# A conditional residual block on one Trainium2 core: the layer norm's square root in another form, small VectorE operations in another order, and b2 by TensorE in other batches

## The chip, the cores and the metric

The kernel runs on one core of a Trainium2 chip. A core has five engines that run side by side, each with its own instructions in order, and that wait for one another by semaphores: TensorE (PE in the profile, PEld for its weight loads), VectorE (DVE), ScalarE (ACT), GpSimd (POOL) and SyncE (SP), which here only issues transfers between memory and the on-chip buffers. TensorE writes to PSUM, a small memory beside the larger SBUF. The metric is the device time of one execution in microseconds (us), lower is better. "Faster" and "slower" compare the changed kernel with the kernel before.

## What is computed

Input x holds 128 batches of 128 rows of 512 numbers (H), in 32-bit floats. For each batch an id from 0 to 8 picks one of ten sets of weights (the gather below), and a small adapter with a layer norm is added to x:

```python
w1 = W1[language_ids]
w2 = W2[language_ids]
h = jnp.einsum('bsh,bha->bsa', hidden_states, w1) + b1[language_ids][:, None, :]
h = jax.nn.relu(h)
adapted = jnp.einsum('bsa,bah->bsh', h, w2) + b2[language_ids][:, None, :]
x = hidden_states + adapted
mean = jnp.mean(x, axis=-1, keepdims=True)
var = jnp.mean(jnp.square(x - mean), axis=-1, keepdims=True)
normed = (x - mean) * jax.lax.rsqrt(var + LN_EPS)
return normed * gamma[language_ids][:, None, :] + beta[language_ids][:, None, :]
```

The result is x plus what this returns. Both products are in 32-bit floats; A, the width of the adapter, is 128.

## The kernel before

A batch (128 rows on the 128 partitions, 512 columns) is the unit of work. All ten W1 and W2 lie in SBUF from the start, and beta, gamma and b2 are spread over the partitions into `beta_b`, `gamma_b` and `b2_b` by products of a 0/1 column of `pick` with `parts` (the rows in three bfloat16 parts), whose results ACT and DVE copy in turn (`spread`).

The order of every engine's instructions is written out by hand: `keep` ties each instruction to the one issued before it on its engine. A loop over i runs one step per batch. In step i the engines work on different batches:

- PE: `transpose_x(i)` (L197, four 128x128 transposes into `pxT`), `down(i-1)` (L220, four products with the batch's W1 copy `w1s`), `up(i-2)` (L237, the product with W2 into `ys[b]`, a PSUM tile `py`). For a batch with `b2_by_matmul(b)` a product with `pick` ahead of it puts b2 into `py` (L236); before, these are batches 0 to 3 and every b with b % 4 == 1.
- ACT: `copy_xT(i)` (L201), `stage_w1(i+1)` (L192), `relu(i-1)` (L228, gives `hT`), `square(i-3)` (L255, the square of y minus mean with the sum over the row as a second output; it takes `nmean` as bias), and after every second batch `deviation` (L261, the square root of variance plus eps for a pair of batches, `sd`).
- POOL: `add_b2(b+2)` (L207, r = x + b2, for the batches whose b2 is not by TensorE) and `add_beta(b)` (L214, o = x + beta), for b = i-3.
- DVE, for b = i-3: `residual(b)` (L243, y = y + r or y + x, with the row sum), `negative_mean(b)` (L248), and for the pair of batches before: the reciprocal square root in five small operations on two columns (`rstd_1` to `rstd_5`, L266, L270, L273, L276, L281: a Newton step on the reciprocal of sd), `scale` (L287, y minus mean, times gamma), `finish` (L296, y times rstd plus o). An even b carries scale of one batch of the pair, rstd_1 to rstd_3 and the finish of the older pair's second batch; an odd b carries rstd_4, the other scale, rstd_5 and the finish of the pair's first batch.
- SP: one load of four batches of x (1 MB) in every fourth step, and one store of two finished batches (512 KB) in every second, in the order of the program.

The buffers that tie engines together: `pxT` and `ph` one each, `py` five, r four, o five pairs, x four groups of four batches. So `up(b)` needs `finish(b-5)` done, and `transpose_x(i+1)` needs the copy of xT i. Batch numbers become weight addresses through registers, which each engine loads for four batches at a time.

The first steps are written apart: products up of batches 0 and 1 before the loop, of batch 2 in step 4, of batch 3 at the end of step 5, behind `down(4)`. The last five batches (E = 123 and up) go through `tail`, which gives the statistics of each batch by itself (`rstd_of`, L317 to L325, `deviation_of`, `shift`), hands three batches to ACT and POOL (`by_pool`) and finishes the last two on DVE (`finish_last`, L357).

Of the kernel before, what the change touches and what calls it, by code (L numbers as in the profile page):

```python
# [8 lines left out]
FP = mybir.dt.float32  # L9
# [7 lines left out]
P = 128  # L17
# [6 lines left out]
def cond_resid_kernel(ctx: ExitStack, tc: tile.TileContext, x, itok, W1, b1, W2, b2, gamma, beta, out):  # L24
# [102 lines left out]
    both = st.tile([P, R], FP, tag="both", name="both", bufs=1)[:96, :]  # L127
    keep(nc.vector.tensor_tensor(both, ident[:96, 0:R], ident[:96, 32 : 32 + R], ALU.add))
    keep(nc.vector.tensor_tensor(pick, both, ident[:96, 64 : 64 + R], ALU.add))


    wrap = const.tile([1, B], I32, name="wrap")
# [51 lines left out]
        return lids[g, engine][b % G]  # L184

    def b2_by_matmul(b):
        return b < 4 or b % 4 == 1

    def stage_w1(b):
        w1s[b] = wp.tile([P, KC, A], FP, tag="w1s", name=f"w1s_{b}")  # L190
# [39 lines left out]
    def up(b):  # L230
# [6 lines left out]
        keep(nc.tensor.matmul(ys[b], lhsT=hT[b], rhs=w2[:, bass.ds(v * H, H)], start=not m, stop=True))  # L237
        del hT[b]

    def residual(b):  # L240
        r = xb(b) if b2_by_matmul(b) else rs.pop(b)
        s = st.tile([P, 1], FP, tag="sum", name=f"sum_{b}")
        keep(nc.vector.scalar_tensor_tensor(ys[b], ys[b], 1.0, r, ALU.mult, ALU.add, accum_out=s))  # L243
        sums[b] = s

    def negative_mean(b):
        nmeans[b] = st.tile([P, 1], FP, tag="nmean", name=f"nmean_{b}")
        keep(nc.vector.tensor_scalar(nmeans[b], sums.pop(b), -1.0 / H, None, ALU.mult))  # L248
# [8 lines left out]
    sds, y0s, stats = {}, {}, {}  # L257

    def deviation(g):
        sds[g] = st.tile([P, 2], FP, tag="sd", name=f"sd_{g}")  # L260
        keep(nc.scalar.activation(sds[g], ssqs[g], AF.Sqrt, bias=eps, scale=1.0 / H))  # L261


    def rstd_1(g):
        stats[g] = p_s.tile([P, 6], FP, tag="s", name=f"stat_{g}")
        keep(nc.vector.tensor_scalar(stats[g][:, 0:2], ssqs.pop(g), -0.5 / H, -0.5 * EPS, ALU.mult, ALU.add))  # L266

    def rstd_2(g):
        y0s[g] = st.tile([P, 2], FP, tag="y0", name=f"y0_{g}")
        keep(nc.vector.reciprocal(y0s[g], sds.pop(g)))  # L270

    def rstd_3(g):
        keep(nc.vector.tensor_tensor(stats[g][:, 2:4], stats[g][:, 0:2], y0s[g], ALU.mult))  # L273

    def rstd_4(g):
        keep(nc.vector.tensor_tensor(stats[g][:, 4:6], stats[g][:, 2:4], y0s[g], ALU.mult))  # L276

    def rstd_5(g):
        rstds[g] = st.tile([P, 2], FP, tag="rstd", name=f"rstd_{g}")
        keep(  # L280
            nc.vector.scalar_tensor_tensor(rstds[g], stats.pop(g)[:, 4:6], 1.5, y0s.pop(g), ALU.add, ALU.mult)  # L281
        )

    def scale(b):
        v = lid(b, ET.DVE)
        keep(
            nc.vector.scalar_tensor_tensor(  # L287
                ys[b], ys[b], nmeans.pop(b), gamma_b[:, bass.ds(v * H, H)], ALU.add, ALU.mult
            )
        )  # L290

# [19 lines left out]
    def rstd_of(b, n):  # L311

        if not ends:
            ends["t"] = p_s.tile([P, 32], FP, tag="s", name="stat_ends")
        t = ends["t"][:, 8 * (b % 4) : 8 * (b % 4) + 3]
        if n == 1:
            keep(nc.vector.tensor_scalar(t[:, 0:1], ssqs.pop(b), -0.5 / H, -0.5 * EPS, ALU.mult, ALU.add))  # L317
        elif n == 2:
            y0s[b] = st.tile([P, 1], FP, tag="y0", name=f"y0_{b}")
            keep(nc.vector.reciprocal(y0s[b], sds.pop(b)))  # L320
        elif n < 5:
            keep(nc.vector.tensor_tensor(t[:, n - 2 : n - 1], t[:, n - 3 : n - 2], y0s[b], ALU.mult))  # L322
        else:
            rstds[b] = st.tile([P, 1], FP, tag="rstd", name=f"rstd_{b}")
            keep(nc.vector.scalar_tensor_tensor(rstds[b], t[:, 2:3], 1.5, y0s.pop(b), ALU.add, ALU.mult))  # L325

    def deviation_of(b):
        ssq = st.tile([P, 1], FP, tag="ssq", name=f"ssq_{b}")
        sq = tp.tile([P, H], FP, tag="sq", name=f"sq_{b}")
        keep(nc.scalar.activation(sq, ys[b], AF.Square, bias=nmeans[b], accum_out=ssq))  # L330
        sds[b] = st.tile([P, 1], FP, tag="sd", name=f"sd_{b}")
        keep(nc.scalar.activation(sds[b], ssq, AF.Sqrt, bias=eps, scale=1.0 / H))
        ssqs[b] = ssq

    def rstd_col(b):
# [24 lines left out]
    def tail(b):  # L360
        p = E // 2
        if b == E + 3:
            rstd_of(b - 2, 4)
        residual(b)
        if b == E + 1:
            rstd_1(p)
            rstd_2(p)
            negative_mean(b)
            rstd_3(p)
            scale(E - 1)  # L370
            rstd_4(p)
            rstd_5(p)
            shift(E)
            finish(E - 2)
            store(p - 1)
            deviation_of(b)
            by_pool(E, False)
        elif b == E + 2:
            negative_mean(b)
            rstd_of(b - 1, 1)  # L380
            rstd_of(b - 1, 2)
            finish_last(E - 1)
            store_last(E)
            rstd_of(b - 1, 3)
            deviation_of(b)
        elif b == E + 3:
            rstd_of(b - 2, 5)
            negative_mean(b)
            shift(b - 2)
            residual(b + 1)  # L390
            negative_mean(b + 1)
            by_pool(b - 2, False)
            store_last(b - 2)
            rstd_of(b - 1, 1)
            rstd_of(b - 1, 2)
            rstd_of(b - 1, 3)
            scale(b - 1)
            deviation_of(b)
            rstd_of(b - 1, 4)
            rstd_of(b - 1, 5)  # L400
# [6 lines left out]
            rstd_of(b + 1, 1)  # L407
            rstd_of(b + 1, 2)
            rstd_of(b, 3)
            rstd_of(b + 1, 3)  # L410
            scale(b + 1)
            rstd_of(b, 4)
            rstd_of(b + 1, 4)
            rstd_of(b, 5)
            rstd_of(b + 1, 5)
            finish_last(b)
            finish_last(b + 1)

# [42 lines left out]
    for i in range(3, B + U):  # L461
        if i < B and i % G == 0 and i // G + 3 < NG:
            load_x(i // G + 3)
        b = i - U - 1
        if i == 4:
            up(2)
        if i > 3 and on(i):
            transpose_x(i)
        if b <= E:
            add_b2(b + 2)  # L470
            add_beta(b)
        if i > 4 and on(i - 1):
# [12 lines left out]
        p = g - 1  # L485
        mine, old = 0 <= p < B // 2, 0 <= p - 1 < B // 2
        if b == E:
            for n in range(b + 3, B):
                add_b2(n)
            for n in range(b + 1, B):  # L490
                add_beta(n)
        if b > E:
            tail(b)
        elif half == 0:
            if on(b):
                residual(b)
# [12 lines left out]
        else:  # L509
            if on(b):  # L510
                residual(b)
            if mine:
                rstd_4(p)
                scale(2 * p + 1)
                rstd_5(p)
# [49 lines left out]
```

## Time and profile before

| | |
|---|---|
| median of 3 runs | 319.38 us (319.27 to 320.71) |
| the profiled execution | 319.72 us |
| its span, first to last instruction | 318.0 us |
| busy: PE, DVE, ACT, POOL | 302.7, 297.9, 289.1, 280.6 us |
| granted TensorE clock, mean | 0.99 |
| HBM read, written | 38.86 MB, 33.55 MB |

An engine's busy time counts overlapping instructions once; it says how much of the span the engine had something in flight, not whether it could have taken more. The groups of the page that the change touches, with line, engine, operation, tiles (out<-in), shape, count, and after the bar the busy time in us, the mean duration of one in ns, and the engine's idle time just before them with what ended most of it:

```profile
L207 POOL TENSOR_TENSOR r<-x,b_b 128x512 f32<-128x512 f32 x93 | 118.9, 1279 | 20.2 <-DMA x<-in_x_dram 12.3
L255 ACT ACTIVATE sq<-py,nmean 128x512 f32<-128x512 f32 x124 | 85.3, 688 | 6.7 <-DVE nmean L248 4.2
L248 DVE TENSOR_SCALAR nmean<-sum 128x1 f32<-128x1 f32 x128 | 18.7, 146 | 0.2
L236 PE MATMUL py<-parts,pick 96*128 96x512 bf16 x35 | 13.3, 381 | 0.0
L276 DVE TENSOR_TENSOR stat<-stat,y 128x2 f32<-128x2 f32 x62 | 12.7, 205 | 0.0
```

The durations of consecutive instructions of one engine overlap, so the sum of durations is more than the time that the engine needs; the distance from one start to the next is the better measure.

### The profile page before, as it was taken

The page shows a single profiled execution, that of the slowest core. Times are in us where ns is not written, and L with a number is a line of the kernel's source. Part 1 is how long each engine was busy: PE and PEld are TensorE (multiplying, and loading weights), DVE is VectorE, ACT ScalarE, POOL GpSimd, SP SyncE. Part 2 cuts the span into 40 slices and gives each one's busy share as a digit, 9 for nine tenths or more (in the row PEclk, how much of TensorE's full clock was granted, in tenths as well). Part 3 has the DMA queues.
Part 4 walks back from the last instruction along what each step waited for, and adds up shares of the span by engine and source line. Part 5 has one row for each costly group of instructions (what it writes and reads, how often), then busy time and mean ns, then how long its engine had stood idle before and what let it go on. Part 6 is the DMA issues. An engine that isn't in the chain of part 4 may idle for free. (4 is left out here: it accounts for less than half of the span.)

```text
span 318.0 us, 7173 instructions
## 1 busy us (share of the span) xinstructions
PE 302.7 (95%) x1883; PEld 225.0 (71%) x1884; DVE 297.9 (94%) x995; ACT 289.1 (91%) x726; POOL 280.6 (88%) x234
## 2 busy tenths in 40 slices
PE   7989999999999999999999999999999999999950
PEld 3566777777777777777777777777777777777730
DVE  6827999999999999999999999999999999999995
ACT  3977999999999999999999999999999999999971
POOL 1308999999999999999999999999999999999873
PEclk9999999999999999999999999999999999999995
DMA  7998777667776666677776666677766666633333
GB/s 204 318 386 294 205 260 262 233 232 266 260 242 212 215 223 242 228 238 265 261 231 215 209 227 248 223 245 264 258 220 208 222 231 241 219 128 133 132 128 138
DMA packets 41002, 72.88 MB, mean 229 GB/s; under 512 B 1753, under 2 KB 6884, under 8 KB 40962
## 3 DMA queue, kind: packets, MB, share of 16 engines
q1 hardware_dynamic: 40902, 72.38, 67.2%
q8 instruction: 15, 0.25, 0.3%
q14 instruction: 25, 0.20, 0.2%
q10 hardware_dynamic: 60, 0.05, 0.1%
HBM read 38.86 MB, written 33.55 MB: 228 GB/s over the span
## 5 line engine op out<-in xcount | busy, mean ns | idle before, releaser
L214 POOL TENSOR_TENSOR o<-x,beta_b 128x512 f32<-128x512 f32 x128 | 162.1, 1280 | 9.2 <-ACT beta_b L164 9.2
L207 POOL TENSOR_TENSOR r<-x,b_b 128x512 f32<-128x512 f32 x93 | 118.9, 1279 | 20.2 <-DMA x<-in_x_dram 12.3
L220 PE MATMUL ph<-xT,w1s 128*128 128x128 f32 x1024 | 135.6, 275 | 0.7 <-ACT w1s L192 0.5
L237 PE MATMUL py<-w,hT 128*128 x256 | 131.0, 594 | 0.9 <-DMA w<-in_L_cond_W_dram 0.7
L220 PEld LDWEIGHTS ph<-xT,w1s 128*128 128x128 f32 x1024 | 124.6, 192 | 2.8 <-ACT hT L228 1.4
L197 PEld LDWEIGHTS pxT<-ident,x 128*128 128x128 f32 x512 | 63.7, 140 | 66.1 <-issue 45.3
L287 DVE SCALAR_TENSOR_TENSOR py<-py,nmean,gamma_b 128x512 f32<-128x512 f32 x126 | 94.6, 751 | 0.0
L255 ACT ACTIVATE sq<-py,nmean 128x512 f32<-128x512 f32 x124 | 85.3, 688 | 6.7 <-DVE nmean L248 4.2
L296 DVE SCALAR_TENSOR_TENSOR o<-py,rstd,o 128x512 f32<-128x512 f32 x122 | 90.3, 740 | 1.0
L192 ACT COPY w1s<-w 128x512 f32 x128 | 79.5, 622 | 0.2 <-DMA w<-in_L_cond_W_dram 0.2
L201 ACT COPY xT<-pxT 128x512 f32<-128x512 f32 x128 | 73.8, 577 | 5.1 <-PE pxT L197 3.6
L197 PE MATMUL pxT<-ident,x 128*128 128x128 f32 x512 | 76.8, 273 | 0.7 <-ACT xT L201 0.7
L243 DVE SCALAR_TENSOR_TENSOR py<-py,r 128x512 f32<-128x512 f32 x93 | 64.4, 692 | 2.5 <-PE pxT L197 0.9
L228 ACT ACTIVATE hT<-ph,b1T 128x128 f32<-128x128 f32 x128 | 47.6, 372 | 1.2 <-PE ph L220 1.2
L237 PEld LDWEIGHTS py<-w,hT 128*128 128x128 f32 x256 | 41.6, 192 | 4.0 <-issue 2.0
L243 DVE SCALAR_TENSOR_TENSOR py<-py,x 128x512 f32<-128x512 f32 x35 | 24.1, 690 | 4.9 <-PE py L237 4.8
L255 ACT ACTIVATION_READ_ACCUMULATOR sq<-py,nmean 128x1 f32 x124 | 24.8, 200 | 0.0
L261 ACT ACTIVATE sd<-ssq,eps 128x2 f32<-128x2 f32 x62 | 18.3, 296 | 2.1
L248 DVE TENSOR_SCALAR nmean<-sum 128x1 f32<-128x1 f32 x128 | 18.7, 146 | 0.2
L236 PE MATMUL py<-parts,pick 96*128 96x512 bf16 x35 | 13.3, 381 | 0.0
L243 DVE DVE_READ_ACCUMULATOR py<-py,r 128x1 f32 x93 | 13.0, 140 | 0.0
L276 DVE TENSOR_TENSOR stat<-stat,y 128x2 f32<-128x2 f32 x62 | 12.7, 205 | 0.0
(54 smaller groups left out, 113.7 us busy)
## 6 DMA issues: line engine op xcount, KB each, us to landing
out_dram<-o SPq DMA_DIRECT2D x61, 512.0 KB, 3.6
x<-in_x_dram SPq DMA_DIRECT2D x30, 1024.0 KB, 6.0
w<-in_L_cond_W_dram SPq DMA_DIRECT2D x4, 640.0 KB, 6.6
w<-in_L_cond_W_dram SPq DMA_DIRECT2D x2, 1280.0 KB, 11.3
x<-in_x_dram SPq DMA_DIRECT2D x4, 512.0 KB, 8.5
out_dram<-o SPq DMA_DIRECT2D x6, 256.0 KB, 2.4
rows<-in_L_cond_beta_dram ACTq DMA_DIRECT2D x1, 20.0 KB
rows<-in_L_cond_gamma_dram SPq DMA_DIRECT2D x1, 20.0 KB
```

What stands on the lines that cost most here:

```text
L192: keep(nc.scalar.copy(w1s[b].rearrange("p k a -> p (k a)"), src))
L197: keep(nc.tensor.transpose(pxs[b][:, k, :], xb(b)[:, k * P : (k + 1) * P], ident))
L201: keep(nc.scalar.copy(xT[b], pxs.pop(b)))
L207: keep(nc.gpsimd.tensor_tensor(rs[b], xb(b), b2_b[:, bass.ds(v * H, H)], ALU.add))
L214: keep(nc.gpsimd.tensor_tensor(os[g][:, j, :], xb(b), beta_b[:, bass.ds(v * H, H)], ALU.add))
L220: nc.tensor.matmul(phs[b], lhsT=w1s[b][:, k, :], rhs=xT[b][:, k, :], start=(k == 0), stop=(k == KC - 1))
L228: keep(nc.scalar.activation(hT[b], phs.pop(b), AF.Relu, bias=b1T[:, bass.ds(lid(b, ET.Activation), 1)]))
L237: keep(nc.tensor.matmul(ys[b], lhsT=hT[b], rhs=w2[:, bass.ds(v * H, H)], start=not m, stop=True))
L243: keep(nc.vector.scalar_tensor_tensor(ys[b], ys[b], 1.0, r, ALU.mult, ALU.add, accum_out=s))
L255: keep(nc.scalar.activation(sq, ys[b], AF.Square, bias=nmeans[b], accum_out=ssqs[g][:, j : j + 1]))
L287: nc.vector.scalar_tensor_tensor(ys[b], ys[b], nmeans.pop(b), gamma_b[:, bass.ds(v * H, H)], ALU.add, ALU.mult)
L296: nc.vector.scalar_tensor_tensor(o, ys.pop(b), rstds[g][:, j : j + 1], o, ALU.mult, ALU.add)
```

## The change

Five parts.

1. `b2_by_matmul`: from batch 4 to 95 the batches whose number leaves 1, 6 or 11 when divided by 16, in place of every fourth; from 96 on every fourth as before. The other batches get b2 from POOL.
2. `up(3)` is called at the start of step 5, ahead of `transpose_x(5)` and `down(4)`, and no longer at its end.
3. The reciprocal square root takes another form, four operations in place of five: the reciprocal of sd, then (ssq + eps) times it, plus sd (Heron's step for the root, twice the root in all), then the reciprocal of that. The factor of two goes into gamma: the columns of `pick` for gamma are multiplied by 2. The small operations are placed so that a 512-column operation stands between each and its input, where there is one: `rstd_1` right behind the even residual, `rstd_2` behind `scale`, `rstd_3` behind `finish`, `rstd_4` behind the odd residual.
4. `square` takes the row sum as bias and -512 as scale (its result is 512 x 512 times the square of before, which the constants of deviation and rstd account for; `H3` is 512 cubed), so it no longer reads `nmean`. Sums and means of two batches lie in one tile of two columns.
5. In `tail` and ahead of it the same operations stand in another order, and `shift` is an operation with a per-row scalar.

```diff
+    keep(nc.vector.tensor_scalar(pick[:, L : 2 * L], pick[:, L : 2 * L], 2.0, None, ALU.mult))
...
     def b2_by_matmul(b):
-        return b < 4 or b % 4 == 1
+        return b < 4 or (b % 16 in (1, 6, 11) if b < 96 else b % 4 == 1)
...
+    def col(tiles, b):
+
+        return tiles[b // 2][:, b % 2 : b % 2 + 1]
+
     def residual(b):
         r = xb(b) if b2_by_matmul(b) else rs.pop(b)
-        s = st.tile([P, 1], FP, tag="sum", name=f"sum_{b}")
-        keep(nc.vector.scalar_tensor_tensor(ys[b], ys[b], 1.0, r, ALU.mult, ALU.add, accum_out=s))
-        sums[b] = s
+        if b % 2 == 0:
+            sums[b // 2] = st.tile([P, 2], FP, tag="sum", name=f"sum_{b // 2}")
+        keep(
+            nc.vector.scalar_tensor_tensor(ys[b], ys[b], 1.0, r, ALU.mult, ALU.add, accum_out=col(sums, b))
+        )
...
-        keep(nc.scalar.activation(sq, ys[b], AF.Square, bias=nmeans[b], accum_out=ssqs[g][:, j : j + 1]))
+        keep(
+            nc.scalar.activation(
+                sq, ys[b], AF.Square, bias=col(sums, b), scale=-float(H), accum_out=col(ssqs, b)
+            )
+        )
...
-        keep(nc.scalar.activation(sds[g], ssqs[g], AF.Sqrt, bias=eps, scale=1.0 / H))
+        keep(nc.scalar.activation(sds[g], ssqs[g], AF.Sqrt, bias=eps, scale=1.0 / H3))
...
     def rstd_1(g):
-        stats[g] = p_s.tile([P, 6], FP, tag="s", name=f"stat_{g}")
-        keep(nc.vector.tensor_scalar(stats[g][:, 0:2], ssqs.pop(g), -0.5 / H, -0.5 * EPS, ALU.mult, ALU.add))
+        y0s[g] = p_s.tile([P, 6], FP, tag="s", name=f"stat_{g}")
+        keep(nc.vector.reciprocal(y0s[g][:, 0:2], sds[g]))
 
     def rstd_2(g):
-        y0s[g] = st.tile([P, 2], FP, tag="y0", name=f"y0_{g}")
-        keep(nc.vector.reciprocal(y0s[g], sds.pop(g)))
+        t = y0s[g]
+        keep(nc.vector.scalar_tensor_tensor(t[:, 2:4], ssqs.pop(g), EPS * H3, t[:, 0:2], ALU.add, ALU.mult))
 
     def rstd_3(g):
-        keep(nc.vector.tensor_tensor(stats[g][:, 2:4], stats[g][:, 0:2], y0s[g], ALU.mult))
+        t = y0s[g]
+        keep(nc.vector.scalar_tensor_tensor(t[:, 4:6], t[:, 2:4], 1.0 / H3, sds.pop(g), ALU.mult, ALU.add))
 
     def rstd_4(g):
-        keep(nc.vector.tensor_tensor(stats[g][:, 4:6], stats[g][:, 2:4], y0s[g], ALU.mult))
-
-    def rstd_5(g):
         rstds[g] = st.tile([P, 2], FP, tag="rstd", name=f"rstd_{g}")
-        keep(
-            nc.vector.scalar_tensor_tensor(rstds[g], stats.pop(g)[:, 4:6], 1.5, y0s.pop(g), ALU.add, ALU.mult)
-        )
+        keep(nc.vector.reciprocal(rstds[g], y0s.pop(g)[:, 4:6]))
...
-    keep(nc.vector.tensor_tensor(ends[b], nmeans.pop(b), rstd_col(b), ALU.mult))
+    keep(nc.vector.tensor_scalar(ends[b], col(nmeans, b), rstd_col(b), None, ALU.mult))
...
         if i == 4:
             up(2)
+        if i == 5:
+            up(3)
         if i > 3 and on(i):
             transpose_x(i)
...
-        if i > 4 and on(i - U):
+        if i > 5 and on(i - U):
             up(i - U)
...
         if b == E:
-            for n in range(b + 3, B):
-                add_b2(n)
-            for n in range(b + 1, B):
+            add_b2(b + 3)
+            add_beta(b + 1)
+            add_b2(b + 4)
+            for n in range(b + 2, B):
                 add_beta(n)
...
             if on(b):
                 residual(b)
             if mine:
+                rstd_1(p)
                 scale(2 * p)
             if on(b):
                 negative_mean(b)
             if mine:
-                rstd_1(p)
                 rstd_2(p)
...
             if mine:
                 rstd_4(p)
                 scale(2 * p + 1)
-                rstd_5(p)
             if on(b):
                 negative_mean(b)
```

In the tail DVE's order after the change is: residual 124, reciprocal of sd for pair 61, scale 122, rstd_2, mean of 124, finish 121, rstd_3, rstd_4, shift 123, residual 125, reciprocal for 124, mean of 125, second step for 124, finish 122, third step, residual 126, last reciprocal for 124, shift 124, residual 127, reciprocal for 125, mean of 126, second step for 125, mean of 127, scale 125, third step and last reciprocal for 125, scale 126, five steps for 126 and 127, scale 127, the last three steps, finish 126, finish 127.

More of the change, by code (lines that the diff above doesn't have):

```diff
@@ L238, in up @@
         del hT[b]
+    def col(tiles, b):
+        return tiles[b // 2][:, b % 2 : b % 2 + 1]
     def residual(b):
         r = xb(b) if b2_by_matmul(b) else rs.pop(b)
-        s = st.tile([P, 1], FP, tag="sum", name=f"sum_{b}")
-        keep(nc.vector.scalar_tensor_tensor(ys[b], ys[b], 1.0, r, ALU.mult, ALU.add, accum_out=s))
-        sums[b] = s
+        if b % 2 == 0:
[3 more added lines that the diff above has]
+        )
     def negative_mean(b):
-        nmeans[b] = st.tile([P, 1], FP, tag="nmean", name=f"nmean_{b}")
-        keep(nc.vector.tensor_scalar(nmeans[b], sums.pop(b), -1.0 / H, None, ALU.mult))
+        if b % 2 == 0:
+            nmeans[b // 2] = st.tile([P, 2], FP, tag="nmean", name=f"nmean_{b // 2}")
+        keep(nc.vector.tensor_scalar(col(nmeans, b), col(sums, b), -1.0 / H, None, ALU.mult))
     def square(b):
@@ L254, in square @@
         sq = tp.tile([P, H], FP, tag="sq", name=f"sq_{b}")
-        keep(nc.scalar.activation(sq, ys[b], AF.Square, bias=nmeans[b], accum_out=ssqs[g][:, j : j + 1]))
+        keep(
[3 more added lines that the diff above has]
+        )
     sds, y0s, stats = {}, {}, {}
+    H3 = float(H) ** 3
     def deviation(g):
         sds[g] = st.tile([P, 2], FP, tag="sd", name=f"sd_{g}")
-        keep(nc.scalar.activation(sds[g], ssqs[g], AF.Sqrt, bias=eps, scale=1.0 / H))
+        keep(nc.scalar.activation(sds[g], ssqs[g], AF.Sqrt, bias=eps, scale=1.0 / H3))
     def rstd_1(g):
-        stats[g] = p_s.tile([P, 6], FP, tag="s", name=f"stat_{g}")
-        keep(nc.vector.tensor_scalar(stats[g][:, 0:2], ssqs.pop(g), -0.5 / H, -0.5 * EPS, ALU.mult, ALU.add))
+        y0s[g] = p_s.tile([P, 6], FP, tag="s", name=f"stat_{g}")
+        keep(nc.vector.reciprocal(y0s[g][:, 0:2], sds[g]))
     def rstd_2(g):
-        y0s[g] = st.tile([P, 2], FP, tag="y0", name=f"y0_{g}")
-        keep(nc.vector.reciprocal(y0s[g], sds.pop(g)))
+        t = y0s[g]
+        keep(nc.vector.scalar_tensor_tensor(t[:, 2:4], ssqs.pop(g), EPS * H3, t[:, 0:2], ALU.add, ALU.mult))
     def rstd_3(g):
-        keep(nc.vector.tensor_tensor(stats[g][:, 2:4], stats[g][:, 0:2], y0s[g], ALU.mult))
+        t = y0s[g]
+        keep(nc.vector.scalar_tensor_tensor(t[:, 4:6], t[:, 2:4], 1.0 / H3, sds.pop(g), ALU.mult, ALU.add))
     def rstd_4(g):
-        keep(nc.vector.tensor_tensor(stats[g][:, 4:6], stats[g][:, 2:4], y0s[g], ALU.mult))
-    def rstd_5(g):
         rstds[g] = st.tile([P, 2], FP, tag="rstd", name=f"rstd_{g}")
-        keep(
-            nc.vector.scalar_tensor_tensor(rstds[g], stats.pop(g)[:, 4:6], 1.5, y0s.pop(g), ALU.add, ALU.mult)
-        )
+        keep(nc.vector.reciprocal(rstds[g], y0s.pop(g)[:, 4:6]))
     def scale(b):
@@ L287, in scale @@
             nc.vector.scalar_tensor_tensor(
-                ys[b], ys[b], nmeans.pop(b), gamma_b[:, bass.ds(v * H, H)], ALU.add, ALU.mult
+                ys[b], ys[b], col(nmeans, b), gamma_b[:, bass.ds(v * H, H)], ALU.add, ALU.mult
             )
@@ L316, in rstd_of @@
         if n == 1:
-            keep(nc.vector.tensor_scalar(t[:, 0:1], ssqs.pop(b), -0.5 / H, -0.5 * EPS, ALU.mult, ALU.add))
+            keep(nc.vector.reciprocal(t[:, 0:1], sds[b]))
         elif n == 2:
[L319 to L322, printed above, removed]
+            keep(
+                nc.vector.scalar_tensor_tensor(t[:, 1:2], ssqs.pop(b), EPS * H3, t[:, 0:1], ALU.add, ALU.mult)
+            )
+        elif n == 3:
+            keep(nc.vector.scalar_tensor_tensor(t[:, 2:3], t[:, 1:2], 1.0 / H3, sds.pop(b), ALU.mult, ALU.add))
         else:
             rstds[b] = st.tile([P, 1], FP, tag="rstd", name=f"rstd_{b}")
-            keep(nc.vector.scalar_tensor_tensor(rstds[b], t[:, 2:3], 1.5, y0s.pop(b), ALU.add, ALU.mult))
+            keep(nc.vector.reciprocal(rstds[b], t[:, 2:3]))
     def deviation_of(b):
@@ L329, in deviation_of @@
         sq = tp.tile([P, H], FP, tag="sq", name=f"sq_{b}")
-        keep(nc.scalar.activation(sq, ys[b], AF.Square, bias=nmeans[b], accum_out=ssq))
+        keep(nc.scalar.activation(sq, ys[b], AF.Square, bias=col(sums, b), scale=-float(H), accum_out=ssq))
         sds[b] = st.tile([P, 1], FP, tag="sd", name=f"sd_{b}")
-        keep(nc.scalar.activation(sds[b], ssq, AF.Sqrt, bias=eps, scale=1.0 / H))
+        keep(nc.scalar.activation(sds[b], ssq, AF.Sqrt, bias=eps, scale=1.0 / H3))
         ssqs[b] = ssq
@@ L362, in tail @@
         if b == E + 3:
-            rstd_of(b - 2, 4)
+            rstd_of(b - 2, 3)
         residual(b)
@@ L366, in tail @@
             rstd_1(p)
+            scale(E - 1)
             rstd_2(p)
             negative_mean(b)
-            rstd_3(p)
-            scale(E - 1)
-            rstd_4(p)
-            rstd_5(p)
-            shift(E)
             finish(E - 2)
             store(p - 1)
+            rstd_3(p)
             deviation_of(b)
+            rstd_4(p)
+            shift(E)
             by_pool(E, False)
         elif b == E + 2:
+            rstd_of(b - 1, 1)
             negative_mean(b)
-            rstd_of(b - 1, 1)
             rstd_of(b - 1, 2)
@@ L383, in tail @@
             store_last(E)
-            rstd_of(b - 1, 3)
             deviation_of(b)
         elif b == E + 3:
-            rstd_of(b - 2, 5)
-            negative_mean(b)
+            rstd_of(b - 2, 4)
             shift(b - 2)
             residual(b + 1)
-            negative_mean(b + 1)
             by_pool(b - 2, False)
@@ L394, in tail @@
             rstd_of(b - 1, 1)
+            negative_mean(b)
             rstd_of(b - 1, 2)
-            rstd_of(b - 1, 3)
+            negative_mean(b + 1)
             scale(b - 1)
             deviation_of(b)
+            rstd_of(b - 1, 3)
             rstd_of(b - 1, 4)
-            rstd_of(b - 1, 5)
             scale(b)
@@ L407, in tail @@
             rstd_of(b + 1, 1)
+            rstd_of(b, 3)
             rstd_of(b + 1, 2)
-            rstd_of(b, 3)
-            rstd_of(b + 1, 3)
             scale(b + 1)
             rstd_of(b, 4)
+            rstd_of(b + 1, 3)
             rstd_of(b + 1, 4)
-            rstd_of(b, 5)
-            rstd_of(b + 1, 5)
             finish_last(b)
@@ L514, in cond_resid_kernel @@
                 scale(2 * p + 1)
-                rstd_5(p)
             if on(b):
```

## The prediction

> **What bounds the kernel now.** I read the page's busy shares first. Four engines stand at 88 to 95% of the span, so they decide nothing; I went on to the timeline of single engines in the middle of the run, where the distance from start to start tells each engine's pace. PE first (start, duration, line, operation, tiles):
>
> ```profile
> 213.93 0.60 PE L197 MATMUL pxT<-ident,x 128*128 128x128 f32 x4
> 214.37 1.06 PE L220 MATMUL ph<-xT,w1s 128*128 128x128 f32 x8
> 215.26 1.02 PE L237 MATMUL py<-w,hT 128*128 x2
> 216.12 0.60 PE L197 MATMUL pxT<-ident,x 128*128 128x128 f32 x4
> ...
> 220.50 0.60 PE L197 MATMUL pxT<-ident,x 128*128 128x128 f32 x4
> 220.94 1.06 PE L220 MATMUL ph<-xT,w1s 128*128 128x128 f32 x8
> 221.83 0.38 PE L236 MATMUL py<-parts,pick 96*128 96x512 bf16 x1
> 222.05 1.02 PE L237 MATMUL py<-w,hT 128*128 x2
> 222.91 0.60 PE L197 MATMUL pxT<-ident,x 128*128 128x128 f32 x4
> ```
>
> A batch takes 2.19 us (213.93 to 216.12): transpose, product down, product up, each starting where the one before has been issued. A batch with b2 by TensorE takes 2.41 (220.50 to 222.91), so that product costs 0.22. The same two distances come back with hardly an exception from batch 6 to batch 124: PE never waits, so it paces the middle. One batch in four has the product: 3 x 2.19 + 2.41 = 8.98 us for four.
>
> DVE is the second. Two consecutive batches:
>
> ```profile
> 105.08 0.75 DVE L287 SCALAR_TENSOR_TENSOR py<-py,nmean,gamma_b 128x512 f32<-128x512 f32 x1
> 105.74 0.15 DVE L248 TENSOR_SCALAR nmean<-sum 128x1 f32<-128x1 f32 x1
> 105.80 0.15 DVE L266 TENSOR_SCALAR stat<-ssq 128x2 f32<-128x2 f32 x1
> 105.86 0.15 DVE L270 RECIPROCAL y<-sd 128x2 f32<-128x2 f32 x1
> 105.94 0.73 DVE L296 SCALAR_TENSOR_TENSOR o<-py,rstd,o 128x512 f32<-128x512 f32 x1
> ...
> 107.99 0.16 DVE L281 SCALAR_TENSOR_TENSOR rstd<-stat,y 128x2 f32<-128x2 f32 x1
> 108.06 0.14 DVE L248 TENSOR_SCALAR nmean<-sum 128x1 f32<-128x1 f32 x1
> 108.24 0.75 DVE L296 SCALAR_TENSOR_TENSOR o<-py,rstd,o 128x512 f32<-128x512 f32 x1
> ```
>
> An operation of 0.15 us occupies only 0.06 when nothing depends on it, and a big one 0.61 to 0.67. L296 at 108.24 waits for rstd, written at 107.99 to 108.15: 0.18 from nmean, not 0.07. A register load in every fourth batch adds 0.12 (L296 to L243 takes 0.79 there, not 0.67). From residual 32 to residual 36, 95.54 to 104.46, four batches take 8.92: DVE just follows PE, its residuals 0.1 to 0.6 us behind the product.
>
> POOL: from 26.59 to 95.57, without one wait, it makes 56 additions, 1.232 us each from start to start. Four batches need seven, 8.62, so it gains on PE and later waits for a free r buffer. ACT makes an xT copy, a w1s copy, hT, the square and its read in 0.47, 0.52, 0.26, 0.57 and 0.11 to 0.25, with the deviation 0.2 to 0.3 more in every second batch: 8.5 us for four.
>
> At the start PE stands still:
>
> ```profile
> 25.74 0.60 PE L197 MATMUL pxT<-ident,x 128*128 128x128 f32 x4
> 27.01 0.66 PE L197 MATMUL pxT<-ident,x 128*128 128x128 f32 x4 [0.68 <-ACT xT L201]
> 27.50 1.06 PE L220 MATMUL ph<-xT,w1s 128*128 128x128 f32 x8
> 28.40 0.38 PE L236 MATMUL py<-parts,pick 96*128 96x512 bf16 x1
> 28.62 1.02 PE L237 MATMUL py<-w,hT 128*128 x2
> 29.48 0.60 PE L197 MATMUL pxT<-ident,x 128*128 128x128 f32 x4
> ```
>
> At the end the chain of waits runs over DVE alone; its shares by engine on the page, and the last entry of DVE's timeline:
>
> ```profile
> DVE 4%; issue 1%; DVEq 0%
> ...
> 313.11 1.41 DVE L357 SCALAR_TENSOR_TENSOR o<-py,rstd,o 128x512 f32<-128x512 f32 x2 [0.39 <-issue]
> ```
>
> [...]
>
> **The change part by part.**
> (1) b2 by TensorE. In batches 4 to 95 it falls from 23 (every fourth) to 17 (three in sixteen); from 96 on it stays 8. PE saves 6 x 0.22 = 1.33 us, all on the path. POOL gets 6 additions more. Sixteen batches now need 29 of them, 29 x 1.232 = 35.73, and PE 16 x 2.19 + 3 x 0.22 = 35.70: level. POOL starts with r of batch 4 ready 5.3 us before its residual, loses about 0.7 of that to the earlier start in (2), and keeps some 4.5 until batch 96; behind it, with one in four, it gains 0.36 on every four batches. From 25.35 it has 99 r and 126 beta additions: 225 x 1.232 = 277.2, so its betas are done at 302.6, before 304.26 today. Cost nothing; the cover is the 4.5 us, which 169 additions up to batch 96 use up if each takes 0.027 more.
>
> (2) Product up of batch 3. It now stands ahead of transpose 5. PE is free at 26.17, when ACT still copies xT 4 (to 26.96). b2 product 26.17 to 26.39, product up 26.39 to 27.25; transpose 5 moves from 27.01 to 27.25, down 4 from 27.50 to 27.69, issued at 28.58. Transpose 6 needs xT 5, which ACT copies at 27.93 to 28.50 after the deviation, as before: it starts at 28.58 where it was 29.48. Gain 0.90. Does ACT follow? Copy of xT 6 at about 30.0 to 30.57, PE asks at 30.77; xT 7 to 32.82, asked at 32.96. Just; I keep 0.90, between 0 (ACT late) and 1.1. A PE wait for a py buffer near batch 19 (0.23) goes too, since DVE gets slack.
>
> (3) Heron's step on DVE. A pair had seven small operations (two nmean, L266, L270, L273, L276, L281), now six. With the distances of the trace, even batch: residual 0.61, scale behind the reciprocal 0.07, 0.66 to nmean, 0.06, 0.07 to L296, 0.65, 0.07 = 2.19; odd batch: 0.61, 0.07, 0.66, 0.07, 0.67 = 2.08. Sum 4.27, with the register load 4.33, against 4.46. PE needs 4.46 for a pair, so this saves nothing in the middle; it only makes room, 0.13 a pair. The new forms (reciprocal into PSUM, two scalar_tensor_tensor on two columns) are not in the trace; the nearest rows are 0.154 to 0.205, and I take 0.07 of engine time each; at 0.12 the pair is 4.47 and the room is gone.
> The reciprocal now stands right behind the even residual and waits there for the deviation (ACT), with the scale, nmean, L296, and so PE's py buffers, queued behind it. At the tightest (batch 120): hT on ACT at 291.80, square 292.07, deviation done at 293.15; product up 120 ends at 292.51, residual from 292.55 to 292.63, reciprocal possible at 293.16 to 293.24. It meets the deviation within 0.02: no cost. At the start it does wait, to 28.06 for pair 0 and about 32.4 for pair 1, while products are still queued in PSUM; buffers for products 6 and 7 come 0.3 and 0.6 us early.
>
> (4) The square's input. It takes the sum, not nmean, so ACT no longer waits for nmean, some 0.8 us later. Off the path until the tail; scale and bias are operands as before. (5) pick x 2 for gamma: one operation like L129 (0.18), covered by the 0.35 that DVE waits for the rows' DMA at L139; 0.2 if uncovered. (6) add_beta ahead of add_b2 at the end: POOL order alone.
>
> (7) The tail. Today residual 124 starts at 301.73 and the last L357 ends at 314.52: 12.79. The new order by the same distances, from residual 124: scale at 0.68, finish 121 at 1.47, two dependent small ones (0.17 each) and the shift to 2.50, residual 125 at 2.57, finish 122 at 3.45, residual 126 at 4.15, shift 124, residual 127 at 5.0, scale 125 at 5.9, scale 126 at 6.8, scale 127 at 8.1 (behind the deviation of 127, ACT), finish 126 at 9.2, end at 10.6. I add 0.4 for a pause like that before L357 (0.39, issue): 11.0. Saved 1.8, between 0.8 (today's pauses stay, or PE's product 127 comes late) and 2.2. PE delivers product 127 at about 304.1 and DVE asks at 304.2, so it fits.
>
> Sum: 1.33 + 0.90 + 0.2 + 1.8 = 4.2. The profiled execution took 319.72 (span 318.0 and 1.7 around it) and would take 315.5; the median of the runs is 319.38, so 315.2.
>
> **Rivals.**
> A, the forecast (0.68): PE paces, 315.2; own range 314.2 to 316.4.
> B (0.20): the ends give less. ACT is too late for transposes 6 to 8 and the tail keeps its pauses: 1.33 + 0.2 + 0.8 = 2.3, 317.0. For it: two margins of 0.2 or less in (2). Against: each is worked out from unhindered ACT distances.
> C (0.06): POOL becomes the bound. At 1.28 us an addition (the page's mean duration) the 169 up to batch 96 take 8.1 longer; less the 4.5 of slack 3.6 are lost: 318.8. For it: 35.73 against 35.70. Against: 56 additions at 1.232 while DVE was as dense.
> D (0.06), slower: the reciprocal of the even batch waits for the deviation in every pair. 62 pairs; 0.13 of wait are hidden, so from 0.20 on (0.07 x 62 = 4.3) the whole gain is lost, and 0.25 gives 322.6. For it: the two meet within 0.02 at best, and ACT has other work. Against: ACT needs 8.5 where PE takes 8.92, so it stays as early as PE lets it.
> That the change does not do what it says is excluded: the changed kernel's instruction order has the six small operations, product 3 ahead of transpose 5, and the fewer products.
>
> **How the numbers follow.** A and B are faster by over 0.5% (under 317.8; half a per cent is about what the measurement tells from no change): 0.88. C is counted as the same, D as slower. Leaving out the fast end of A, C's far half and D, the range is 314.0 to 317.4.
>
> **What would show it.** Right: transposes 2.19 and 2.41 apart, transpose 6 near 28.6, transpose 124 near 292.3 (294.76 today); POOL almost without waits; residual 124 to the last finish in about 11 us. Wrong: a repeated DVE wait for sd ahead of the reciprocal (D), DVE waiting for r from POOL (C), transposes 6 to 8 waiting for xT (B), or PE waiting for finish.

## The result and the profile after

The changed kernel is slower: median 322.81 us of six runs (322.46 to 325.78) against 319.92 us of six of the kernel before on the same chip (319.27 to 321.06), ratio 1.0105, 95% interval 1.0063 to 1.0148. The forecast was 315.2. The profiled execution is the slowest of the six (325.78 us, span 324.0), so what its lines show is two to three us larger than in the median run. Two kernels below, e8 and e11, ran in two groups of times about 2% apart, the kernel before only in one; where e11 is compared, its lower group is.

The clock is no cause: the granted clock is 1.00 from 16 to 310 us in both profiles. What the profile shows first is that the chain of waits, followed back from the end, has changed its engine. Chain of the changed kernel, shares by engine:

```profile
POOL 44%; PE 29%; issue 12%; DMA 3%; POOLq 3%; SPq 3%; DVE 1%; ACT 1%; ACTq 0%
```

POOL now has the largest share of it. The groups and DMA issues that say why (busy time and mean ns, then idle time before and its releaser; for the DMA the median time from issue to landing):

```profile
L239 PE MATMUL py<-w,hT 128*128 x256 | 131.9, 597 | 3.2 <-DVE o L309 2.5
...
L216 POOL TENSOR_TENSOR o<-x,beta_b 128x512 f32<-128x512 f32 x128 | 162.6, 1281 | 19.7 <-DMA out_dram<-o 10.5
...
L251 DVE SCALAR_TENSOR_TENSOR py<-py,r 128x512 f32<-128x512 f32 x99 | 68.9, 696 | 11.2 <-POOL r L209 8.6
...
out_dram<-o SPq DMA_DIRECT2D x61, 512.0 KB, 7.2
```

Read from the third line's releaser back: DVE waits for r from POOL, POOL waits for an o pair to be stored, and PE in turn waits for DVE's finish to free a py buffer. POOL's addition itself takes no longer than before (1281 ns mean, 1.23 from start to start). Before, a store landed 3.6 us after its issue (median), now 7.2. The waits of SP, which issues them (total us, times, longest), first before, then after:

```profile
SPq L300 <- DVE stat L273: 217.0, 60, 4.6
SPq L67 <- DVE py L243: 20.5, 27, 11.4
SPq L67 <- POOL o L214: 8.1, 6, 2.7
```

```profile
SPq L67 <- POOL o L216: 165.7, 26, 9.2
SPq L313 <- DVE stat L291: 48.1, 17, 4.2
```

Before, SP spent its time in front of a store (L300), waiting for the two batches to be finished: whatever came ready went out. After, it spends it in front of a load (L67), waiting for POOL to give a slot of x free, and the stores stand behind that load. SP's timeline in the changed kernel, in the middle of one such period, and POOL's first addition that waits (last column: idle time before, and its releaser):

```profile
47.03 0.37 SPq L313 DMA_DIRECT2D out_dram<-o  x1
47.94 8.35 SPq L67 DMA_DIRECT2D x<-in_x_dram  x2
56.38 4.39 SPq L313 DMA_DIRECT2D out_dram<-o  x3
```

```profile
63.42 1.27 POOL L216 TENSOR_TENSOR o<-x,beta_b 128x512 f32<-128x512 f32 x1 [1.40 <-DMA out_dram<-o]
```

The first of the two loads leaves at 47.94, the second, after waiting for POOL, at 55.90, and for 9 us, from 47.40 to 56.38, no store leaves. A pair is finished about every 4.5. This row of two loads comes six times, once in sixteen batches up to batch 96, and each ends in a POOL wait for a store: 1.40, 3.24, 1.67, 1.33, 1.33 and 1.54 us.

POOL cannot escape this wait by being early, because the sequence starts from POOL itself. Each time the second load leaves 0.02 to 0.03 us behind POOL's beta addition for the last batch of the old group (here batch 15, which ends at 55.88), and the store leaves 0.5 to 0.9 us behind the load. POOL asks for the stored pair 5.3 to 5.7 us after the store's issue and goes on 6.9 to 8.9 us after it. Had the store landed in 3.6 us as before, POOL would have found the pair free (an estimate from these distances): the store is late in its issue and slow in its landing, and the wait needs both.

The order of SP's instructions in the two kernels (L a load of four batches, s a store of a pair; the part from step 8):

```
before   L s s  L s s  L s s  L s s  L s s  L s s  L s s ...
after    L s s s  L L s s s  L s s  L s s s  L L s s s ...
```

In every sixteen batches, the load of step 12 goes behind a store and the store of step 15 goes behind the load of step 16. No line of the change touches SP. But the stores are the one instruction of the loop that `keep` does not tie (the section on the kernel before said that every engine's order is written out; for these it is not), so the kernel leaves their place open, and it came out another when one line that does not concern SP was changed (e3 below).

Where the six us of span went, from the starts of transposes and last instructions of the profiles (e1 is the changed kernel with its stores tied, below):

| stretch, us | before | after | e1 |
|---|---|---|---|
| start to transpose 4 | 25.74 | 25.68 | 25.49 |
| transpose 4 to 96 | 206.15 | 207.52 | 204.14 |
| transpose 96 to 124 | 62.87 | 63.91 | 62.87 |
| transpose 124 to the end of DVE's last finish | 19.76 | 18.48 | 18.32 |
| from there to the end | 3.48 | 8.41 | 3.38 |
| span | 318.0 | 324.0 | 314.2 |

The largest piece against e1, 5.0 us, is at the very end: POOL, late since batch 18, ends its addition for batch 127 at 313.02 (before 304.26), then its last two additions at 319.37, and the last stores follow.

### The profile page after: what moved, and what is told of

The parts are those of the page before. It is cut to its first block, busy times and chain, and to the rows that moved or that the text cites. A ratio compares the mean times of both kernels' runs of the same rounds, so it can differ in the third digit from the quotient of the medians.

```text
span 324.0 us, 7096 instructions
## 1 busy us (share of the span) xinstructions
PE 303.6 (94%) x1878; PEld 224.2 (69%) x1878; DVE 291.7 (90%) x930; ACT 287.9 (89%) x726; POOL 287.1 (89%) x240
## 4 chain that ended last, share of the span: by engine, by line
POOL 44%; PE 29%; issue 12%; DMA 3%; POOLq 3%; SPq 3%; DVE 1%; ACT 1%; ACTq 0%
POOL o L216 24%; POOL r L209 19%; PE py L239 12%; PE ph L222 11%; PE pxT L199 6%; DMA w<-in_L_cond_W_dram 3%; SPq L98 2%; POOLq L176 2%; SPq L84 1%; POOL o L364 1%; POOL n L362 1%; POOLq L216 1%; PE py L238 1%; POOLq L209 1%; POOLq L571 0%
## 5 line engine op out<-in xcount | busy, mean ns | idle before, releaser
L216 POOL TENSOR_TENSOR o<-x,beta_b 128x512 f32<-128x512 f32 x128 | 162.6, 1281 | 19.7 <-DMA out_dram<-o 10.5
L209 POOL TENSOR_TENSOR r<-x,b_b 128x512 f32<-128x512 f32 x99 | 126.9, 1281 | 11.9 <-DMA x<-in_x_dram 11.9
L300 DVE SCALAR_TENSOR_TENSOR py<-py,nmean,gamma_b 128x512 f32<-128x512 f32 x126 | 93.8, 744 | 0.0
L266 ACT ACTIVATE sq<-py,sum 128x512 f32<-128x512 f32 x124 | 85.3, 688 | 7.5 <-DVE rstd L295 4.1
L251 DVE SCALAR_TENSOR_TENSOR py<-py,r 128x512 f32<-128x512 f32 x99 | 68.9, 696 | 11.2 <-POOL r L209 8.6
L266 ACT ACTIVATION_READ_ACCUMULATOR sq<-py,sum 128x1 f32 x124 | 25.4, 205 | 0.0
L251 DVE SCALAR_TENSOR_TENSOR py<-py,x 128x512 f32<-128x512 f32 x29 | 20.2, 695 | 4.0 <-PE py L239 3.8
L251 DVE DVE_READ_ACCUMULATOR py<-py,r 128x1 f32 x99 | 14.1, 142 | 0.0
L283 DVE RECIPROCAL stat<-sd 128x2 f32<-128x2 f32 x62 | 12.8, 207 | 1.1 <-ACT sd L277 1.1
L238 PE MATMUL py<-parts,pick 96*128 96x512 bf16 x29 | 11.0, 381 | 0.0
```

Of the source, the lines that this page charges most:

```text
L209: keep(nc.gpsimd.tensor_tensor(rs[b], xb(b), b2_b[:, bass.ds(v * H, H)], ALU.add))
L216: keep(nc.gpsimd.tensor_tensor(os[g][:, j, :], xb(b), beta_b[:, bass.ds(v * H, H)], ALU.add))
L266: nc.scalar.activation(sq, ys[b], AF.Square, bias=col(sums, b), scale=-float(H), accum_out=col(ssqs, b))
L300: nc.vector.scalar_tensor_tensor(ys[b], ys[b], col(nmeans, b), gamma_b[:, bass.ds(v * H, H)], ALU.add, ALU.mult)
```

## The experiments

The theory: SP's order makes the stores late, the five o pairs pass that to POOL, and POOL, which has no room, to DVE and PE. Rivals: POOL is simply loaded too much (29 additions in 16 batches), the new DVE order costs, or the two loads side by side do. No kernel below leaves out or changes any part of the computation.

**e1, stores in order.** The changed kernel, with both stores tied; only SP's order differs.

```diff
-        nc.sync.dma_start(out=out[2 * g : 2 * g + 2].rearrange("b s h -> s b h"), in_=os.pop(g))
+        keep(nc.sync.dma_start(out=out[2 * g : 2 * g + 2].rearrange("b s h -> s b h"), in_=os.pop(g)))
```

> The changed kernel with SP's stores kept in the order of the program (load, store, store, as before), nothing else. Theory O (SP's order): in the changed kernel two loads stand together once in sixteen batches, the second waits for POOL, and a store that POOL's next beta needs stands behind it; with the order restored POOL no longer waits for stores and PE paces: 315.0 to 316.5 us. Theory P (POOL's 29 additions per sixteen batches are too many by themselves): no change, 321 to 323. Theory H (DVE's new order holds it up): no change.

Measured: 316.04 (315.95 to 316.36), ratio to the kernel before 0.9888 (0.9866 to 0.9909). SP's timeline over the same stretch, POOL's wait for stores, and the chain:

```profile
47.75 0.38 SPq L67 DMA_DIRECT2D x<-in_x_dram  x1
48.17 3.65 SPq L313 DMA_DIRECT2D out_dram<-o  x2
54.66 0.38 SPq L67 DMA_DIRECT2D x<-in_x_dram  x1
55.82 4.75 SPq L313 DMA_DIRECT2D out_dram<-o  x2
```

```profile
POOL o L216 <- DMA out_dram<-o: 0.5, 1, 0.5
```

```profile
PE 86%; DMA 4%; DVE 3%; SPq 3%; ACT 2%; issue 1%; DVEq 1%; ACTq 0%
```

The store that this kernel issues at 51.44 is the one that the changed kernel issues at 56.38. With it in time POOL waits for a store once, for 0.5 us, PE paces to batch 124, and the change is a gain. So neither the load on POOL nor DVE's order makes the changed kernel slower. This is the fastest version but for differences of 0.2 us, and it beats both kernels.

**e2, b2 every fourth.** The changed kernel with the old pattern; SP's order is then the old one.

```diff
-        return b < 4 or (b % 16 in (1, 6, 11) if b < 96 else b % 4 == 1)
+        return b < 4 or b % 4 == 1
```

> The changed kernel with b2 by TensorE in every fourth batch as before; SP's order is then load, store, store by itself. Theories O and P: PE does six products more than in the first run, 1.33 us, so 316.5 to 317.8 us, POOL waiting for r buffers only. Theory H: still 321 to 323.

Measured: 317.91 (316.96 to 318.13), 0.9936 (0.9916 to 0.9957). POOL waits for no store; it waits for free r buffers, 6.4 us in 21 times, which is room. The pattern is worth 317.91 - 316.04 = 1.87 us where the order is kept, and in the profiles, transpose 4 to 124, 268.32 - 267.01 = 1.31.

**e3, the pattern alone.** The kernel before with the new `b2_by_matmul` and nothing else.

> The kernel before with the new choice of b2 batches alone; SP's order becomes that of the changed kernel. Theories O and P: as slow as the changed kernel or slower, 322 to 325 us, POOL waiting for stores once in sixteen batches. Theory H: 318 us, since only PE's six products go.

Measured: 326.66 (326.17 to 326.97), 1.0212 (1.0189 to 1.0234). SP's order is that of the changed kernel, and POOL waits for stores:

```profile
POOL o L214 <- DMA out_dram<-o: 8.7, 6, 1.7
```

So this one line of the change brings the reordering. That it costs more than in the changed kernel does not come from the middle (transpose 4 to 124 takes 270.41 us, in the changed kernel 271.43), but from one operation of the old tail:

```profile
305.19 6.10 DVE L340 TENSOR_TENSOR shift<-nmean,rstd 128x1 f32<-128x1 f32 x1
306.32 4.95 POOL L214 TENSOR_TENSOR o<-x,beta_b 128x512 f32<-128x512 f32 x4
```

The old `shift` multiplies two one-column operands in SBUF, and here it ends at 311.29, 0.02 us behind the last of POOL's beta additions (311.27). In the kernel before, e4, e8 and e11 it ends 0.02 behind that addition too, but after 0.46 or 0.47 us, since POOL is nearly done when it starts. The new form, with a per-row scalar, takes 0.21 in every run that has it, also in the changed kernel, where POOL makes beta additions until 313.02. So this part of the change, which the prediction does not price, keeps POOL's lateness off DVE in the tail.

**e4, SP's order alone.** The kernel before, its stores tied, with the changed kernel's SP order written out.

```diff
+        if i % 16 == 12 and i < 96:
+            late.append(i // G + 3)
-        if i < B and i % G == 0 and i // G + 3 < NG:
+        elif i < B and i % G == 0 and i // G + 3 < NG:
             load_x(i // G + 3)
+        while held and i % 16 == 0:
+            store(held.pop())
...
-                store(p - 1)
+                if i % 16 == 15 and i < 96:
+                    held.append(p - 1)
+                else:
+                    store(p - 1)
+                while late and i % 16 == 13:
+                    load_x(late.pop())
```

> The kernel before with SP's order of the changed kernel written out, nothing else; POOL has 28 additions in sixteen batches, and up to 9 us of advance. Theory O: POOL needs 34.5 us for sixteen batches and can lose 1.3 before it meets PE's 35.9, so stores come late but the time stays within 319 to 320.5 us: order and POOL's full load must come together. If the order is harmful by itself: 321 or more. Theory P: no change.

Measured: 321.79 (321.57 to 322.31), 1.0070 (1.0047 to 1.0093). POOL's waits for stores are there:

```profile
POOL o L214 <- DMA out_dram<-o: 9.0, 6, 2.5
```

But POOL, with one addition less in sixteen batches than in the changed kernel, makes them good, as expected: r is ready at least 6.7 us before its residual all through this profile. What PE loses between transposes 8 and 124, 1.5 us (0.3 before), lies four to six batches behind four long distances from a finish to the next residual on DVE: 1.68, 1.11, 1.15 and 1.14 us, where 0.8 is usual. The longest:

```profile
103.50 0.75 DVE L296 SCALAR_TENSOR_TENSOR o<-py,rstd,o 128x512 f32<-128x512 f32 x1
105.18 0.70 DVE L243 SCALAR_TENSOR_TENSOR py<-py,r 128x512 f32<-128x512 f32 x1 [0.92 <-PE ph L220]
```

At this place DVE loads the batch numbers of four batches into registers, and this load took 1.50 us (median of the run 0.63). So the time was missed for another reason than a wait for POOL. Before, there are three long distances too, up to 1.23. Whether SP's order lengthens the register loads is not shown.

**e5 and e6, which half of the order.** Both start from e1. e5 puts only the store of step 15 behind the load of step 16 (the `held` lines of e4), e6 only the load of step 12 behind the store of step 13 (the `late` lines).

> The first run's kernel (stores in order), with one store in sixteen batches (that of step 15) put behind the load of step 16; the load of step 12 stays in time. Theory O1 (the store behind a load that waits for POOL's beta of batch 15 is what costs): POOL waits over 0.8 us for that store once in sixteen batches, 319 to 322.5 us. Theory O2 (two loads next to each other, and so transfers in a bunch, are what costs): 316.0 to 316.8.

> The first run's kernel with the other half of the reordering: the load of step 12 behind the store of step 13, all stores in time. Theory O1: 315.9 to 316.8 us, the load has some 15 us to spare. Theory O2: between this and the changed kernel, 318 to 321.

Measured: e5 323.40 (323.03 to 325.76), 1.0106 (1.0089 to 1.0123), e6 315.93 (315.72 to 316.09), 0.9872 (0.9856 to 0.9889). e5 is the changed kernel over again, down to POOL's wait:

```profile
POOL o L216 <- DMA out_dram<-o: 10.5, 6, 3.1
```

The load that comes later does no harm; the store behind a waiting load is all of it, 323.40 - 315.93 = 7.5 us for six stores. Nor is it the two loads side by side: e5 has a store between them and is slow, e7 has them side by side and is not.

**e7, a sixth o pair.** The changed kernel, its SP order as it came, with one buffer more.

```diff
-    op = ctx.enter_context(tc.tile_pool(name="op", bufs=5))
+    op = ctx.enter_context(tc.tile_pool(name="op", bufs=6))
```

> The changed kernel with SP's bad order left as it is and six pairs of o in place of five. If the wait goes through the o buffers (store late, buffer late, beta late): POOL asks for a buffer two batches later, 4.4 us, its waits of 1.3 to 3.2 us go, and the time is 316.0 to 317.0 us. If the late loads or the bunched transfers themselves hold POOL or PE: 319 or more.

Measured: 315.84 (315.49 to 315.96), 0.9866 (0.9850 to 0.9883); no POOL wait for a store. So the late store hurts through the o ring alone. **e12** is e1 with the sixth pair:

> The changed kernel with the stores in order and six pairs of o: both remedies together. One wait for a store of 0.5 us is left in the first run; it goes. PE paces: 315.5 to 316.1 us, not to be told from the first, sixth and seventh run.

Measured: 316.10 (315.98 to 316.30), 0.9879 (0.9856 to 0.9901). With the order kept, the pair is worth nothing.

**e8 and e11, the pattern in the kernel before, order kept.** e8 is e3 with the stores tied, e11 is e8 with six o pairs. Does the new pattern pay without the new DVE order?

> The kernel before with the new choice of b2 batches and SP's stores kept in order; DVE, the start and the tail as before. By the prediction's sum the pattern is worth 1.33 us and POOL is level: 318.0 to 318.6 us beside 319.5. If DVE of before cannot follow PE at the new pace (8.92 us for four batches against 8.925): up to 319.5.

> The eighth run's kernel (before, new b2 choice, stores in order) with six pairs of o. If its slow runs came from POOL waiting for o (1.2 us in its trace): 318.0 to 318.6 us. If they came from DVE, which at PE's new pace has no room for register loads of up to 1.5 us: again 319.5 to 328 us, with distances of 1.1 us and more from finish to residual in every fourth batch.

Measured: e8 325.85, 328.31, 319.57 and 327.60, too uneven for a ratio. e11 six times 319.14 to 319.58 and eleven times 325.1 to 328.15; the lower group against the kernel before 0.9987 (0.9974 to 1.0001). In a profile of that group, transpose 9 to 96 takes 194.08 us (before 195.62) and 96 to 124 takes 63.76 (62.87): more than half of what PE saves is given back behind batch 96. The profile of e8 is of the upper group (325.85). In it DVE takes more than 1.05 us from finish to residual in 13 of the 29 batches in which a register load stands there, up to 1.65 (three times before, twice in the profile of e11), and PE loses 6.3 us between transposes 8 and 124 (0.3 before, 0.9 in e11). In e1, with the new DVE order, the one such distance, 1.21, costs PE nothing. This suggests that the old order has no room for long register loads; why some executions have so many of them stays open.

**e9 and e10, the other parts.** e9 is e1 with product up 3 at its old place; e10 is the changed kernel with the old b2 pattern and product 3 at its old place, so that the DVE order and the tail are left.

```diff
-        if i == 5:
-            up(3)
...
-        if i > 5 and on(i - U):
+        if i > 4 and on(i - U):
```

> The first run's kernel (stores in order) with the product up of batch 3 at the end of step 5 as before. The trace of the first run has transpose 7 at 30.95 us where before has 31.66, from starts of transpose 4 of 25.49 and 25.74: 0.46 gained. So 316.4 to 316.7 us. If the prediction's 0.90 is right: 316.9. If other engines take the gain back: 316.0.

> The changed kernel with the b2 choice of before and product 3 late as before: only Heron's step, the square's input, the order on DVE and the tail are changed; SP's order is that of before by itself. By the prediction: tail 1.8 and 0.2 in the middle, 317.5 us beside 319.5 to 320.0. If the tail gives 1.3 as the first run's trace has it (11.47 us against 12.79) and the middle nothing: 318.3 to 318.8. If DVE's room brings nothing at all: 319.5 to 320.

Measured: e9 316.65 (316.52 to 316.75), 0.9895 (0.9874 to 0.9917), so product 3 is worth 0.6 (e1 has 316.04, e12, on the same chip as e9, 316.10); e10 318.47 (318.31 to 318.57), 0.9956 (0.9936 to 0.9976), so DVE's part with the tail is worth 1.2.

## Why the prediction was wrong

**The step that failed** is in part (1): "Cost nothing; the cover is the 4.5 us". It weighed POOL's own rate, 29 additions of 1.232 against PE's 35.70, and the additions did not get slower. But it took POOL's inputs and buffers as they were before. It followed what the change moves on PE, DVE, ACT and POOL, and not on SP, whose stores are not tied; the new pattern brought another order of SP with it, which put one store in sixteen batches behind a load (e3, e5). One late store costs POOL 1.3 to 3.2 us, and as POOL's sixteen batches are level with PE's, nothing is made good: POOL's lead, from r ready to its residual, shrinks from 5.1 us at batch 4 to 0.1 at batch 37, and from there the period of sixteen is 37.12 us (POOL's waits end at 139.89, 177.02 and 214.14) where PE needs 35.70. The 4.5 us of cover stood against six waits of 10.5 in all, and what the step put at nothing cost about 7 us (2.2% between the ratios 1.0105 of the changed kernel and 0.9888 of e1). With the stores in order the working of (1) holds: in e1 the lead is 6.2 at batch 4 and 5.0 at batch 96.

The other steps, with SP's order kept (e1), where they can be read:

- **(1), the 1.33 us of PE**: right, 1.31 between e2 and e1. That it is "all on the path" holds only with the new DVE order: in e11, with the old one, no gain clear of the noise is left.
- **(2), 0.90**: mis-sized. Transpose 6 starts at 28.33 (predicted 28.58), but by transpose 7 only 0.46 is left (30.95 for 31.66, of which 0.25 was there at transpose 4), and e9 puts it at 0.6. The working asked whether ACT copies xT in time and left out that down 5 needs `ph`, of which there is one, so it waits until ACT has read it for hT 4 (from the profile of e1):

```profile
28.33 0.63 PE L199 MATMUL pxT<-ident,x 128*128 128x128 f32 x4
28.67 0.37 ACT L230 ACTIVATE hT<-ph,b1T 128x128 f32<-128x128 f32 x1
29.09 1.16 PE L222 MATMUL ph<-xT,w1s 128*128 128x128 f32 x8
```

  By the usual distance PE could take down 5 at 28.77, 0.44 behind the transpose; hT ends at 29.04. That is most of what is missing. The small gain near batch 19 (0.2) was there: from transpose 7 to 96 it is 231.89 - 31.66 = 200.23 before and 229.63 - 30.95 = 198.68 in e1, so 1.55 saved, 1.33 and 0.22.
- **(3), a pair in 4.27**: right; the distances in e1 sum to 4.28, and each new two-column operation holds DVE for 0.06 to 0.08. PE, not DVE, paces e1 to batch 124, as said.
- **(4) and (6), nothing**: no cost is seen; the square takes 689 ns in the mean in e1, 688 before. POOL's last beta addition ends at 301.72 (predicted 302.6). **(5)**: not seen apart; transpose 4 comes 0.25 earlier, not later.
- **(7), the tail in 11.0**: mis-sized. It takes 11.47 (299.35 to 310.82), so 1.3 is saved and not 1.8. The pause before L371 did not come, but the one-column operations on the tile `stat_ends` follow one another at 0.20, where 0.17 and 0.07 were reckoned, and this also where one does not use the other's result, as here the third step for batch 126 behind the first for 127:

```profile
307.73 0.17 DVE L330 RECIPROCAL stat_ends<-sd 128x1 f32<-128x1 f32 x1
307.93 0.17 DVE L336 SCALAR_TENSOR_TENSOR stat_ends<-stat_ends,sd 128x1 f32<-128x1 f32 x1
```

- **The sum**: 4.2 was said; with SP's order kept (e1) it is 319.54 - 316.04 = 3.5.
- **The rivals**: C named the right engine, at a chance of 0.06, but by another way (an addition of 1.28 in place of 1.232), and it ended at no change. D did not come: the reciprocal waits for sd once, at the start, 1.1 us. B's ends did give less than A's, but by 0.7 and not by 1.9. The sign was wrong because no rival had a late store in it.

The signs to watch did name what came, "DVE waiting for r from POOL" and "PE waiting for finish", but as the mark of a slow POOL. The releaser of POOL's own wait, a store, told the two apart.

## What to carry to other kernels

In a kernel whose order is written by hand, look for the instructions that are not tied, and compare the order of every queue before and after a change, those that only issue DMAs too. SP's queue, which issues loads and stores in turn, passed a load's wait for POOL (up to 9.2 us in the changed kernel) on to the store behind it. Where one engine releases such a load and soon needs the buffer that this store frees, being early does not save it from the wait: here the load left 0.02 to 0.03 us behind POOL's addition every time, so an earlier POOL would only have moved the whole sequence. A change that takes an engine to the same rate as the one that paces also takes away its power to catch up, so price such stalls at their full length, less the lead that is there: at 29 additions in sixteen batches, level with PE, 10.5 us of waits cost about 7, and in e4, with one addition less, POOL made 9.0 us of them good.

## What the runs showed of the hardware

- The same 512 KB store landed later where it was issued close behind a 1 MB load. Of the stores between 30 and 270 us whose landing the profiles show, four after that left 0.47 us behind a load landed in 6.1 to 7.3 us, seven in e1 that left within 0.6 us of one in 6.8 to 8.5, and nine before that left 7.3 to 8.5 us behind one in 3.1 to 3.7. The distance is not all of it: at 3.0 to 3.8 us behind a load, nine before landed in 3.6 to 4.5 and three after in 6.6 to 8.8. Nor does SP's order alone decide it: the medians are 3.6 before, 6.0 in e1 with the same order, 7.2 after, and 3.2 in e4 with the order of after.
- In the tails before, after and of e1, a one-column VectorE operation took, from its start to the next one's, 0.06 to 0.08 us at the least where the next did not use its result, 0.12 to 0.15 in other such places, and 0.19 to 0.21 where the next used it. Operations of the new kernel on different columns of `stat_ends` followed at 0.20 too (e1, 307.73 and 307.93).
- The first L340 on VectorE, an operation on two one-column operands in SBUF, ended 0.02 us behind POOL's last beta addition in all five profiles that have it, once after 6.10 us (e3); with a per-row scalar it took 0.21 while POOL went on adding.
- The register load of four batch numbers on VectorE took 0.34 to 1.05 us before (median 0.61), 0.34 to 1.07 after (median 0.71), and up to 1.50 in e4, where the residual behind it started 1.68 us after the finish ahead of it, at a usual 0.8.
